# Three float16 casts at three places of ScalarE's queue, and one VectorE subtraction behind the factors of the tangent sums

## The chip, the cores and the metric

The kernel runs on one core of one Trainium2 chip. The metric is the device time of one launch in microseconds (us), of which the shorter is the better. A core has TensorE (PE in the profile, for matmuls and transposes), VectorE (DVE), ScalarE (ACT), GpSimd (POOL) and SyncE (SP, which here only issues the loads). Each takes its instructions from a queue of its own, in order[...].

## The reference, cut to what matters

Four graph layers follow each other over x (4096 nodes by 64 features) and a dense 0/1 adjacency of 4096 by 4096. Each ends in `x = layernorm(x + layer(x, adj))`. Layer 0 is a mean over neighbours with a linear map. Layer 2 is a sum over neighbours with weights that halve with each further neighbour. Layers 1 and 3 are the same hyperbolic attention:

```python
adj_att = sigmoid(left[:, None] + right[None, :] + b) * adj   # left, right: x_tan @ w
x_local = _logmap(x[:, None, :], x[None, :, :])               # 4096 x 4096 x 64
support = einsum('ij,ijd->id', adj_att, x_local)
return _proj(_expmap(x, support))
```

`_logmap` of a pair depends on x_i, x_j and their dot product. The kernel gets that dot product, together with terms of the two norms, from TensorE: a vector y (x times a factor of its norm) is split into a float16 upper half and a float16 lower half (y minus the upper half), and the products of the halves are summed in PSUM. `left` and `right` need a logarithm per node, and the sums over neighbours run over x times factors of its norm, which the kernel holds in `xe`.

## The kernel before, in words

**Tiling.** The 4096 nodes lie in 32 blocks of 128 (P). Destination columns come in four groups of 1024, walked from 3 down to 0 (`GROUPS`); source blocks come two at a time, also downwards. For each group and pair of blocks, SyncE loads 1 MB of the adjacency (L698) into one of six `edges` buffers, so that the adjacency is read once for each layer, 256 loads in all.

**Four stages.** In layer 0, TensorE sums neighbours (L1414). In layers 1 and 3 (`attend`, L1025) each pair of a block and a group has six matmuls into a PSUM tile z (L1059, L1062, L1065), a sigmoid and a square on ScalarE (L1074, L1077), two or three passes on VectorE (L1080, L1082) and, for a pair of blocks, eight matmuls into acc (L1037). Layer 2 is one wide pass over the groups 3 and 2 and then a narrow pass each for group 1 and group 0. In a narrow pass each block adds to two z tiles in place (four matmuls, L1569), ScalarE takes two exponentials of them (L1576), and four matmuls add up the result one block later (L1581). The next block's count into a z tile can't begin before the exponential has read it.

**Rows.** When a group of a layer has been summed, its 1024 rows become the next layer's x: `end_0` (L1357) or `end_2` (the function with L1494 to L1504), `norm_rows` (L862), and `prepare` (L882), the part that the change touches. `prepare` works out the norm's terms and y (L896), and leaves the rest to a generator, `second`, which is put into a queue of small steps. In its order: the three casts of y on ScalarE (L899 and L900 into two places of `ys`, L901 into `yd`); the terms of the norm in float16 (L903 to L914, on VectorE and GpSimd); the lower half of y (L915, on VectorE, which reads the result of L899); the factors and `xe` (L918 to L923); the inputs of the logarithms (L926 to L931); then four rounds that each transpose eight blocks of `ys` or `yd` into PSUM (L943) and copy them out on ScalarE (L947) as `hi_lo`, `lo_hi`, `src` and `dst`; the two logarithms (L950, L951); the product with the attention vectors (L955); and the small operations that give `left` and `right` (L965 to L977). In this text a chain is one run of `second`, named by the group of rows it works on. An attention over any destination group needs the chain of source group s only when it comes to the blocks of s.

**What sets the order.** `tick` (L614) is called between the main steps: four times for each load in layer 0, once for each block in the narrow passes. It lets the generators at the heads of two queues go on. `yield n` means: not before n ticks from now. `second` stands in the second queue, and a generator runs to its end before the next one in that queue starts:

```python
for queue in queues:
    while queue and queue[0][1] <= place[1]:
        wait = next(queue[0][0], None)
        ...
        queue[0][1] = place[1] + wait
        if wait:
            break
```

In layers 0 and 2 the main loops stand in `with tc.manual_schedule(engines=FIXED)`, where FIXED is PE and ACT: these two keep the order in which the program wrote them. VectorE and GpSimd are ordered by a list scheduler. In layers 1 and 3 it orders all engines. It also moves instructions that are written after the block of layer 2 forward into that stage: three sigmoids of layer 3's first group stand there among the exponentials of the last narrow pass. Where ScalarE goes over from exponentials to logarithms or sigmoids, or back, the built program has an ACT_TABLE_LOAD; copies, casts and squares stand among all three without one.

**PSUM.** Transposes use one `aux` tile; in layer 2 half of a third z tile serves as a second one (`take`, L667, alternates), which is given back at the end of the stage (`spare_ends`, L676).

Of the kernel before, what the change touches and what calls it, by code (L numbers as in the profile page):

```python
# [21 lines left out]
D = 64  # L22
# [36 lines left out]
def gnn_stack_kernel(  # L59
# [16 lines left out]
    V = nc.vector  # L76
# [492 lines left out]
    def stream(fits):  # L569

        with ExitStack() as st:
# [130 lines left out]
            def grp(name, bufs=None):  # L702
                kw = {"bufs": bufs} if bufs else {}
                return row.tile([P, WB, D], F32, name=name, **kw)

            def nums(name, n=WB):
                return row.tile([P, n], F32, name=name)

            def over(v):
                return v[:, :, None].to_broadcast([P, v.shape[1], D])  # L710
# [87 lines left out]
            ys = keep.tile([P, WB, 3 * D + 10], F16, name="ys")  # L798
# [83 lines left out]
            def prepare(layer, s, att, b_att, curve, least, good, small):  # L882
# [11 lines left out]
                ym, y = nums("ym"), grp("y")  # L894
# [2 lines left out]

                def second():
                    nc.scalar.copy(ys[:, :, :D], y)  # L899
                    nc.scalar.copy(ys[:, :, 2 * D : 3 * D], y)  # L900
                    nc.scalar.copy(yd[:, :, :D], y)  # L901
                    hl = row.tile([P, WB, 2], F16, name="hl")
                    V.tensor_scalar(hl[:, :, 0], rbg, UNIT, None, ALU.mult)  # L903
# [7 lines left out]
                    for k, of in ((7, 0), (8, 0), (9, 1)):  # L911
                        nc.gpsimd.tensor_scalar(
                            ed[:, :, k], hl[:, :, of], -2.0 / UNIT, None, ALU.mult
                        )  # L914
                    V.tensor_sub(ys[:, :, D : 2 * D], y, ys[:, :, :D])  # L915

                    m, g, w = nums("m"), nums("g"), grp("xw")
                    V.tensor_scalar(g, cx2[:, at], 1.0, 1.0 / D, ALU.add, ALU.mult)  # L918
# [2 lines left out]
                    V.tensor_add(w, xg, over(g))  # L921
                    yield 1
                    V.tensor_mul(xe[:, at, :], w, over(m))  # L923

                    q, q1, t = nums("q"), nums("q1"), nums("tt")
                    V.tensor_scalar(q, x2[:, at], least, c, ALU.max, ALU.mult)  # L926
# [63 lines left out]
                    yield 1  # L990

                later(second(), True, after(small))
                yield 1

# [714 lines left out]
```

## Time and profile before

| What | us |
|---|---|
| median of three runs (1107.23 to 1113.71) | 1108.87 |
| the profiled execution: its own time | 1108.28 |
| its span, first to last instruction | 1106.6 |
| busy PE, DVE, ACT, POOL | 1001.9, 915.5, 803.1, 273.1 |
| layer 0 (to about 190.6) | 190.6 |
| layer 1 (to about 517) | 326.4 |
| layer 2: wide pass, narrow pass of group 1, narrow pass of group 0 (ends at 759.28) | 110.2, 61.2, 70.9 |
| layer 3 | 347.7 |
| one cast (L899, L900, L901), eight of each | 0.62 |
| one ACT_TABLE_LOAD, 19 ahead of L950, L1074 and L1576 | 1.28 |
| lower half of y (L915), eight | 0.69 |

The time of one launch is the span plus 1.7 us around it. Times "at 737" are us from the span's start. A row of the timeline has the start, the busy time, the engine, the line, the operation with its output and input, how many instructions are merged, and in brackets the idle time of the engine ahead of it with what ended it. Rows of one engine can overlap by about 0.1 us[...].

### The profile page before, as it was taken

To read this page: it belongs to the slowest core of one execution; us is meant where nothing else is said; L and a number is where in the kernel's file an instruction comes from. 1 tells how busy PE (TensorE), PEld (TensorE's weight loads), DVE (VectorE), ACT (ScalarE), POOL (GpSimd) and SP (SyncE) were. 2 spreads that over 40 slices of the span, in tenths; PEclk is the share of its full clock that TensorE was granted. 3 is DMA by queue.
4 is the path that set the end of the run, shared out by engine and by line. 5 is a ranking of instruction groups with operands and counts; after the bars stand their busy time and mean duration, and the time that the engine had idled before them with its cause. 6 is when DMAs were issued, how large, how long until landed. Compare 5 with 4: busy or idle time off the path is not lost.

```text
span 1106.6 us, 13832 instructions
## 1 busy us (share of the span) xinstructions
PE 1001.9 (91%) x4949; PEld 392.4 (35%) x4949; DVE 915.5 (83%) x1452; ACT 803.1 (73%) x892; POOL 273.1 (25%) x649
## 2 busy tenths in 40 slices
PE   4998998889999999998998998789899999999980
PEld 2454554333333333332333332223333333333320
DVE  5777977989999999999456484545999999999996
ACT  0003123879999999897676788889899998998960
POOL 0011212010144443525500010000001444346173
PEclk8999999889999999999998999799999999999995
DMA  9999999536565565654877987477545656666400
GB/s 341 378 419 380 370 423 396 190 131 244 191 240 219 188 238 219 228 194 148 333 304 275 362 289 261 155 270 285 203 169 211 251 214 229 228 227 227 164 1 23
DMA packets 38581, 271.63 MB, mean 245 GB/s; under 512 B 4710, under 2 KB 4710, under 8 KB 5734
## 3 DMA queue, kind: packets, MB, share of 16 engines
q1 hardware_dynamic: 37728, 270.03, 64.8%
q8 instruction: 41, 0.67, 0.2%
q10 hardware_dynamic: 774, 0.63, 0.2%
q14 instruction: 38, 0.31, 0.1%
HBM read 269.58 MB, written 1.05 MB: 245 GB/s over the span
## 4 chain that ended last, share of the span: by engine, by line
PE 55%; DVE 24%; ACT 9%; DMA 5%; POOL 3%; issue 2%; ACTq 0%; SPq 0%; POOLq 0%; DVEq 0%
PE acc L1037 15%; PE z L1569 9%; DVE t L1082 7%; PE z L1059 7%; PE z L1065 6%; PE z L1062 6%; DVE t L1080 6%; DMA edges<-in_adj_dram 4%; PE acc L1581 3%; PE acc L1414 3%; ACT sq L1077 3%; ACT sq L1576 2%; DVE junk L838 2%; ACT sig L1074 1%; PE z L1581 1%
## 5 line engine op out<-in xcount | busy, mean ns | idle before, releaser
L1080 DVE SCALAR_TENSOR_TENSOR t<-z,sig 128x1024 f32<-128x1024 f32 x256 | 308.8, 1217 | 13.0 <-ACT sq L1077 6.8
L1077 ACT ACTIVATE sq<-z,turn 128x1024 f32<-128x1024 f32 x256 | 277.8, 1111 | 45.1 <-PE z L1065 18.4
L1082 DVE SCALAR_TENSOR_TENSOR t<-sq,t 128x2048 f32<-128x2048 f32 x128 | 297.3, 2322 | 0.5
L1074 ACT ACTIVATE sig<-left_b,right 128x1024 f32<-128x1024 f32 x256 | 285.9, 1146 | 1.9 <-DVE t L1080 1.3
L1037 PE MATMUL acc<-t,xe 128*64 128x512 f32 x1024 | 255.2, 608 | 17.2 <-DVE t L1082 16.8
L1059 PE MATMUL z<-edges,two_i 128*128 128x512 bf16 x512 | 201.2, 393 | 7.4 <-DVE t L1080 7.4
L1065 PE MATMUL z<-dst,src 74*128 74x512 f16 x512 | 195.5, 382 | 0.0
L1062 PE MATMUL z<-lo_hi,hi_lo 128*128 128x512 f16 x512 | 194.4, 380 | 0.0
L1576 ACT ACTIVATE sq<-z,at_edge 128x512 bf16<-128x512 f32 (+1 forms) x192 | 149.3, 828 | 46.0 <-PE z L1569 43.5
L838 DVE SCALAR_TENSOR_TENSOR t<-edges 128x2048 bf16<-128x2048 f32 x32 | 73.0, 2287 | 54.2 <-DMA edges<-in_adj_dram 54.2
L1037 PEld LDWEIGHTS acc<-t,xe 128*64 128x64 f32 x1024 | 63.8, 136 | 145.6 <-issue 83.8
L1569 PE MATMUL z<-edges,pass_by 128*128 128x512 bf16 x248 | 89.5, 401 | 17.9 <-ACT sq L1576 17.8
L1414 PE MATMUL acc<-edges,first 128*128 128x512 bf16 x256 | 80.1, 394 | 17.6 <-DMA edges<-in_adj_dram 17.3
L1059 PEld LDWEIGHTS <-two_i 128*128 128x128 bf16 x512 | 50.3, 98 | 128.9 <-issue 82.3
L1569 PE MATMUL z<-edges,enter 128*128 128x512 bf16 x256 | 91.0, 398 | 0.0
L1414 PE MATMUL acc<-edges,third 128*65 128x512 bf16 x256 | 80.0, 394 | 0.0
L838 DVE SCALAR_TENSOR_TENSOR junk<-edges 128x2048 bf16<-128x2048 f32 x32 | 73.1, 2286 | 4.7 <-DMA edges<-in_adj_dram 4.4
L1065 PEld LDWEIGHTS <-src 74*128 74x128 f16 x512 | 49.2, 96 | 70.5 <-issue 8.0
L1062 PEld LDWEIGHTS <-hi_lo 128*128 128x128 f16 x512 | 50.4, 98 | 57.1 <-issue 11.7
L1581 PE MATMUL acc<-sq,halves 128*64 128x512 bf16 x384 | 62.5, 403 | 1.0 <-ACT sums L1088 0.8
L869 POOL TENSOR_TENSOR sq<-z 128x512 f32<-128x512 f32 x8 | 14.2, 1776 | 164.3 <-DVE z L868 132.2
L1133 POOL TENSOR_TENSOR w_att<-x,u 128x512 f32<-128x512 f32 x6 | 15.6, 2595 | 141.2 <-ACT u L1128 141.2
(375 smaller groups left out, 940.9 us busy)
## 6 DMA issues: line engine op xcount, KB each, us to landing
edges<-in_adj_dram SPq DMA_DIRECT2D x256, 1024.0 KB, 4.7
x<-in_x_dram SPq DMA_DIRECT2D x4, 256.0 KB
out_dram<-x ACTq DMA_DIRECT2D x2, 256.0 KB
out_dram<-x SPq DMA_DIRECT2D x2, 256.0 KB
w_sb<-in_L_gnn_W_dram ACTq DMA_DIRECT2D x1, 32.0 KB, 4.8
w_twice<-in_L_gnn_weight_dram ACTq DMA_DIRECT2D x2, 16.0 KB, 8.6
given<-in_L_gnn_b_dram ACTq DMA_DIRECT2D x1, 0.2 KB
given<-in_L_gnn_bias_dram ACTq DMA_DIRECT2D x1, 0.2 KB
```

The source lines that it names most:

```text
L838: V.scalar_tensor_tensor(junk, a, 0.0, a, ALU.not_equal, ALU.not_equal, accum_out=odd[:, n : n + 1])
L1037: it = nc.tensor.matmul(acc[h * D : (h + 1) * D, :], xe[:, j, :], t[:, k, h * W : (h + 1) * W], start=j == BLOCKS[0], stop=j == BLOCKS[-1],)
L1059: nc.tensor.matmul(half, two_i, edge[:, at : at + W], start=True, stop=False)
L1062: nc.tensor.matmul(half, hi_lo[:, of], lo_hi[:, to], start=False, stop=False)
L1065: last = nc.tensor.matmul(half, src[:, of], dst[:, to], start=False, stop=True)
L1074: nc.scalar.activation(sig, left_b, AF.Sigmoid, bias=right[:, j : j + 1])
L1077: nc.scalar.activation(sq[:, k], zp, AF.Square, bias=turn, scale=-1.0 / UNIT)
L1080: V.scalar_tensor_tensor(t[:, k], zp, 0.0, sig, ALU.max, ALU.mult)
L1082: V.scalar_tensor_tensor(t, sq, HIGH**2, t, ALU.add, ALU.mult)
L1414: nc.tensor.matmul(accs[h][:m], lhs[:, j, :], edge[:, at : at + W], start=j == BLOCKS[0], stop=j == BLOCKS[-1],)
L1569: nc.tensor.matmul(z[:, h : h + W], lhs, rhs[:, h : h + W], start=j == BLOCKS[0], stop=True, skip_group_check=True,)
L1576: nc.scalar.activation(w, z[:, :n], AF.Exp, bias=at_edge, scale=-LN2)
```

## The change

`second` gives up its turn after each of the first two casts, so that the three casts come at three ticks rather than at one, and everything behind them comes two ticks later. The subtraction for the lower half of y is written behind the product that gives `xe`.

```diff
                 def second():
                     nc.scalar.copy(ys[:, :, :D], y)
+                    yield 1
                     nc.scalar.copy(ys[:, :, 2 * D : 3 * D], y)
+                    yield 1
                     nc.scalar.copy(yd[:, :, :D], y)
                     hl = row.tile([P, WB, 2], F16, name="hl")
                     V.tensor_scalar(hl[:, :, 0], rbg, UNIT, None, ALU.mult)
...
-                    V.tensor_sub(ys[:, :, D : 2 * D], y, ys[:, :, :D])

                     m, g, w = nums("m"), nums("g"), grp("xw")
...
                     V.tensor_add(w, xg, over(g))
                     yield 1
                     V.tensor_mul(xe[:, at, :], w, over(m))
+                    V.tensor_sub(ys[:, :, D : 2 * D], y, ys[:, :, :D])
```

No instruction is added to or taken from the source; the lines below L899 move down by one or two in the changed file. Lines in the text are those of the kernel before.

## The prediction

> **What bounds the kernel now.** The page's busy shares (PE 91%, DVE 83%, ACT 73%) are averages over stages with different limits, so I first asked for the windows of the passes of layer 2, where `prepare` runs beside exponentials, and of the first stretch of layer 3. The columns are the window, its length, and busy time with instruction counts.
>
> ```profile
> core 0: us, PE busy (x) PEld busy (x) DVE busy (x) ACT busy (x) POOL busy (x), PEclk, DMA share, GB/s
> 640.89:688.40 47.51, 42.47 (x240) 14.20 (x239) 32.41 (x113) 39.12 (x62) 5.55 (x15) 0.96 0.76 276
> 688.40:759.28 70.88, 59.07 (x334) 19.86 (x334) 28.83 (x87) 63.28 (x91) 2.39 (x8) 0.90 0.63 227
> 759.28:797.48 38.20, 34.59 (x151) 12.09 (x150) 36.66 (x66) 33.05 (x34) 1.55 (x2) 1.00 0.62 228
> ```
>
> In the pass of group 0 (second row) ScalarE is busy for 63.3 of 70.9 us and VectorE for 28.8: ScalarE and TensorE share the limit and VectorE has room. In the stretch behind it VectorE is busy for 36.7 of 38.2 us and sets the pace.
>
> Second, ScalarE's timeline at the chain of group 1:
>
> ```profile
> 735.71 1.26 ACT L1576 ACTIVATE sq<-z,at_edge 128x512 bf16<-128x512 f32 x2 [0.30 <-PE z L1569]
> 736.86 0.62 ACT L899 CAST ys<-y 128x512 f16<-128x512 f32 x1
> 737.37 0.63 ACT L900 CAST ys<-y 128x512 f16<-128x512 f32 x1
> 737.89 0.62 ACT L901 CAST yd<-y 128x512 f16<-128x512 f32 x1
> 738.41 1.27 ACT L1576 ACTIVATE sq<-z,at_edge 128x512 bf16<-128x512 f32 x2
> 739.87 1.27 ACT L1576 ACTIVATE sq<-z,at_edge 128x512 bf16<-128x512 f32 x2 [0.19 <-PE z L1569]
> ```
>
> An undisturbed block takes 1.57 us (exponentials at 734.15 and 735.71), in which ScalarE works for 1.27 and waits 0.30 for z. The three casts put 1.55 us between two blocks. On TensorE's timeline:
>
> ```profile
> 739.16 0.39 PE L1569 MATMUL z<-edges,pass_by 128*128 128x512 bf16 x1 [0.97 <-ACT sq L1576]
> ```
>
> Third, the chain of group 2's logarithms, and the end of the pass, where group 1's stand:
>
> ```profile
> 723.68 1.27 ACT L1576 ACTIVATE sq<-z,at_edge 128x512 bf16<-128x512 f32 x2
> 724.97 1.28 ACT L950 ACT_TABLE_LOAD   x1
> 726.26 0.21 ACT L950 ACTIVATE tt<-tt 128x8 f32<-128x8 f32 x1
> 726.38 0.19 ACT L951 ACTIVATE q<-q 128x8 f32<-128x8 f32 x1
> 726.59 1.28 ACT L1576 ACT_TABLE_LOAD   x1
> ```
> ```profile
> 759.29 1.28 ACT L950 ACT_TABLE_LOAD   x1
> 760.59 0.21 ACT L950 ACTIVATE tt<-tt 128x8 f32<-128x8 f32 x1
> 760.70 0.19 ACT L951 ACTIVATE q<-q 128x8 f32<-128x8 f32 x1
> 760.80 0.56 ACT L1610 COPY sums<-acc 128x512 f32<-128x512 f32 x1
> ```
>
> Inside the pass two logarithms cost two table loads, and the next exponential starts at 727.88, 4.20 us after the last instead of 1.57: 2.63 lost. At the end they come behind the last exponential, and their second load is the sigmoids', needed anyway.
>
> **What the Trainium skill says.** "ScalarE: Activation LUTs", section "What ACT_TABLE_LOAD costs", gives about 1283 ns for the load and 1380 for a drain, 2.66 us for a switch. The trace agrees on the load (1283 ns) and not on the drain: the load starts 0.02 us after the exponential, the logarithm 1.29 later, so I price a switch at 1.29. The section "Table sets: the hidden batching unit" says to batch functions by set. "Perfetto Trace Analysis", section "Optimizing Scalar/DVE Operations", says that where ScalarE causes bubbles on other engines, breaking work up may free them sooner; the 0.97 us above is such a bubble. "TensorE: Matmul & The Clock Gate", section "What's actually happening", has a gate pass only part of the clock by how busy TensorE has been. The granted clock was 0.75 in 700 to 720, behind the three hoisted sigmoids.
>
> **The change part by part.** I read the order of the built programs, engine by engine.
>
> *VectorE's subtraction: 0.* It costs 0.69 us wherever it stands. The list scheduler already put it behind `xe` in layer 0 (L923 at 84.95, L915 at 85.64). Its one stall, 3.69 us on L899 at 737.5, fell where VectorE had work for 28.8 of 70.9 us. Its cover gone, it would cost up to 0.69 per chain, bounds 0 and +0.7 (only the last chain, in layer 3, lies where VectorE is full).
>
> *Layer 0: 0, bounds -2 and +2.* DMA is 0.96 busy up to 190.6. Group 3's `lo_hi` copy (1.01) moves behind the four copies of sums, and group 2's rows no longer wait 1.62 us for the logarithm at 105.7. SyncE's loads do wait for L838 on VectorE, so the cover isn't perfect. Layer 1's order and the last three groups of layer 3 are unchanged, and so are the orders on POOL and SP: no DMA is moved past anything.
>
> *Casts, three chains in layer 2: -1.4.* One block apart, each of three blocks takes 1.27 + 0.52 = 1.79, 0.22 over 1.57: 0.66 for three. Group 1 lost 1.02 before (2.70 and 1.46 for two blocks, less 2 x 1.57): gain 0.36. Group 2's casts lie among table loads, where ScalarE never waits: 1.27 + 1.55 + 2 x 1.57 = 5.96 becomes 3 x 1.79: gain 0.6. Group 3 lost 1.8, of it 0.66 waiting for y, which stays, then 0.22 twice: gain 0.5. Bounds: -3.5 (all of it hidden) and 0. In layer 3 the scheduler keeps the casts together: 0.
>
> *The queue: six blocks.* Chains follow each other in one queue, so the two ticks add up: group 3's ends two blocks later, group 2's four, group 1's begins four and ends six later. Before, group 1's chain left the pass with its last block. Now it begins eight blocks ahead of the end, and two of its copies, its logarithms and L955 are written behind the manual block. The scheduler moves the two logarithms forward, singly: load, L950, load, one block, load, L951, load, with the last three blocks still to come behind. Each is 1.28 + 0.2 + 1.28, say 2.85 with the start-up, less 0.30 of idle time: 2.5. Two: +5.0. Bounds: +4.2 (one more idle gap hidden each) and +5.3 (2.63 each).
>
> *TensorE's clock behind them: +1.2.* After the logarithms at 669 the next blocks took 1.85 and 2.49, 1.2 over, with matmuls at 0.63 instead of 0.39; after those at 726 nothing. Two interruptions one block apart resemble the sigmoids at 689 to 705, which were followed by a dip. Bounds 0 and +2.4; I take one dip.
>
> *Transposes that leave the pass: -1.4.* A block with transposes took 2.05 us (exponentials at 748.71 and 750.76): 0.48 over. Three of group 1's four rounds now fall at or behind the last block. Bounds -1.4 and 0, since they go into layer 3.
>
> *The end of the pass: 0.* From the last exponential's end (759.28) to the first L1080 (762.82) it was 3.54. Now the sums' copy can start when acc is done (+0.95, so +1.5), but the `lo_hi` copy (0.9) must free the one `aux` tile before the transposes of the sums (0.6) and L1494 (0.34): about 3.5 again. Bounds -1 and +1.5.
>
> *VectorE in layer 3: +0.9.* L965, L968, L975 to L977, L983, L988 and L989 of group 1 stood at 758.9 to 762.2, beside the wait; now they stand between L1080s: eight times about 0.11. Bounds 0.6 and 1.2, unless L965 has to wait (rival B).
>
> *Group 0's chain in layer 3: +0.5.* Casts and copies come two squares earlier, and the table load for its logarithms catches VectorE with one sigmoid in hand rather than two. Bounds -1 and +2.
>
> Sum: -1.4 + 5.0 + 1.2 - 1.4 + 0.9 + 0.5 = +4.8. On the profiled execution, 1108.28 (span 1106.6 and 1.7 around it), that is 1113.1; on the median, 0.6 higher, 1113.7, which I give.
>
> **Rivals.**
>
> B, the other side of the line, slower at 1118: L965 waits on VectorE for L955, which waits for the `dst` copy to free `aux`, behind two squares, a table load, a sigmoid, the `src` copy and a square on ScalarE. I place that at 10.7 us behind the last exponential, and VectorE gets there at 11.4. Past 0.7 us of delay each us is paid in full, since all L1080s queue behind L965; a trip of transpose and copy more (0.6 + 0.9), twice, gives 3, with a second dip 4.2: 1113.7 + 4.2. For it: one tile where there were two. Against: ScalarE had 5 us of idle time up to 797.
>
> C, a gain: the moved work is hidden, the casts free their whole 3.5 and layer 0 gains 2, while the loads cost 4.2: 1107. For it: L838 holds loads. Against: the 2.63 at 726, measured in this very place.
>
> D, the change doesn't do what it says: spreading frees nothing and the logarithms' loads are absorbed by the six blocks' freedom: 1109. Against: ScalarE's built order has three more table loads in a pass where it is 89% busy.
>
> **How the numbers follow.** Chances: my forecast A 0.50, B 0.20, C 0.15, D 0.15. Anything within 0.5% (5.5 us) can't be told from no change by a measurement of this kernel. A spreads over 1110 to 1117 and lies beyond 1114.4 with 0.18 of its 0.50. Slower: 0.18 + 0.20 = 0.38. Faster: 0.04 of C and 0.01 of D, 0.05. Within: 0.57. The range from 1107.5 to 1119 leaves out most of C's gains and B's tail.
>
> **What would show it.** Right: ten table loads in the last narrow pass become thirteen; two gaps of about 2.3 us on L1569; no gap of 0.97 at the casts; the pass of group 0 longer by 3 to 5 us, layers 0 and 1 unchanged. Wrong: the loads cost under 1 us each on TensorE, VectorE idles at L965, or layer 0 ends at another time by over 2 us.

## The result, and the profile after

The changed kernel takes 1123.26 us, the median of six runs (1116.48 to 1125.64), beside 1108.22 for the kernel before. The ratio of the two sets of runs is 1.0111, 95% interval 1.0084 to 1.0138, or some 12 us; the quotient of the two medians alone would be 1.0136. I had forecast 1113.7 and a range up to 1119. The profiled execution, one of the quicker of the six, has 1118.83, 10.55 more than the 1108.28 of before, and its span is 1117.1: the stretches below account for these 10.5 us, not for the whole distance of the medians. A later comparison of the same kernel gave 1.0109 (1.0070 to 1.0148).

To say where the time went I cut both spans at three events that every trace has: the copy of the wide pass's sums in layer 2, the end of the last exponential, and the copy of layer 3's first sums.

| Stretch, us | before | after | difference | my forecast |
|---|---|---|---|---|
| start to the wide pass's sums | 625.51 | 623.09 | -2.4 | 0 |
| the two narrow passes, to the last exponential | 133.77 | 137.84 | +4.1 | +3.4 |
| from there to layer 3's first sums | 92.18 | 98.13 | +5.9 | +1.4 |
| the rest of layer 3 | 255.14 | 258.04 | +2.9 | 0 |
| span | 1106.6 | 1117.1 | +10.5 | +4.8 |

The narrow passes went as I had worked out, and the stretch behind them did not. First, ScalarE's timeline at the logarithms of group 1, which answers to the third block of the prediction (start, busy time, operation, idle time before it). Rows carry the line numbers of the file that ran: in the changed kernel L952, L953, L967, L1496 and L1578 are L950, L951, L965, L1494 and L1576 of the kernel before.

```profile
744.43 1.30 ACT L1578 ACTIVATE sq<-z,at_edge 128x512 bf16<-128x512 f32 x2
745.76 1.28 ACT L952 ACT_TABLE_LOAD   x1
747.05 0.21 ACT L952 ACTIVATE tt<-tt 128x8 f32<-128x8 f32 x1
747.28 1.28 ACT L1578 ACT_TABLE_LOAD   x1
748.57 1.27 ACT L1578 ACTIVATE sq<-z,at_edge 128x512 bf16<-128x512 f32 x2
749.86 1.28 ACT L953 ACT_TABLE_LOAD   x1
751.15 0.21 ACT L953 ACTIVATE q<-q 128x8 f32<-128x8 f32 x1
751.38 1.28 ACT L1578 ACT_TABLE_LOAD   x1
752.67 1.27 ACT L1578 ACTIVATE sq<-z,at_edge 128x512 bf16<-128x512 f32 x2
754.12 1.27 ACT L1578 ACTIVATE sq<-z,at_edge 128x512 bf16<-128x512 f32 x2 [0.18 <-PE z L1571]
757.38 1.48 ACT L1578 ACTIVATE sq<-z,at_edge 128x512 bf16<-128x512 f32 x2 [1.99 <-PE z L1571]
...
759.65 1.28 ACT L1578 ACTIVATE sq<-z,at_edge 128x512 bf16<-128x512 f32 x2
```
```profile
749.31 0.39 PE L1571 MATMUL z<-edges,pass_by 128*128 128x512 bf16 x1 [2.36 <-ACT sq L1578]
753.41 0.39 PE L1571 MATMUL z<-edges,pass_by 128*128 128x512 bf16 x1 [2.36 <-ACT sq L1578]
```

Each of the two interruptions holds TensorE for 2.36 us, and two blocks behind the second ScalarE waits 1.99 us for z. The windows of the last narrow pass, of the stretch up to group 0's y, and of the pass's last 8.9 us show the granted clock (the number before the DMA share): it has fallen to 0.81 at the end of the pass, and the matmuls of the z that ScalarE waits for take 0.63 us instead of 0.39.

```profile
core 0: us, PE busy (x) PEld busy (x) DVE busy (x) ACT busy (x) POOL busy (x), PEclk, DMA share, GB/s
684.27:760.93 76.66, 59.89 (x304) 19.39 (x308) 29.89 (x100) 67.07 (x95) 3.14 (x8) 0.89 0.62 210
760.93:800.27 39.34, 36.63 (x165) 13.37 (x167) 34.64 (x62) 33.02 (x33) 1.51 (x2) 0.96 0.63 224
752.00:760.93 8.93, 7.52 (x41) 2.85 (x40) 0.16 (x1) 6.63 (x10) 0.00 (x0) 0.81 0.49 175
```

The second row answers to the third of the prediction's first block: the stretch has grown from 38.2 to 39.3 us, and VectorE works in it for 34.6 us where it worked for 36.7 (one pass of L1082, 2.2 us, now comes behind y). VectorE's timeline at the end of the pass, first before:

```profile
761.82 0.16 DVE L976 TENSOR_TENSOR right<-lr,f 128x8 f32<-128x8 f32 x1
...
762.15 0.42 DVE L1494 SCALAR_TENSOR_TENSOR z<-aux,given_b 128x256 f32<-128x256 f32 x1
762.49 0.41 DVE L1498 SCALAR_TENSOR_TENSOR z<-aux,given_b 128x256 f32<-128x256 f32 x1
762.82 1.21 DVE L1080 SCALAR_TENSOR_TENSOR t<-z,sig 128x1024 f32<-128x1024 f32 x1
...
810.14 0.21 DVE L965 TENSOR_REDUCE lr<-aux 128x16 f32<-128x48 f32 x1
```

and then after, with one row of GpSimd:

```profile
764.59 0.42 DVE L1496 SCALAR_TENSOR_TENSOR z<-aux,given_b 128x256 f32<-128x256 f32 x1 [12.43 <-PE aux L1097]
764.93 1.22 DVE L1082 SCALAR_TENSOR_TENSOR t<-z,sig 128x1024 f32<-128x1024 f32 x1
766.07 0.41 DVE L1500 SCALAR_TENSOR_TENSOR z<-aux,given_b 128x256 f32<-128x256 f32 x1
...
773.09 1.08 POOL L869 TENSOR_TENSOR sq<-z 128x512 f32<-128x512 f32 x1 [48.58 <-DVE lr L967]
773.18 1.01 DVE L978 TENSOR_TENSOR right<-lr,f 128x8 f32<-128x8 f32 x1
...
813.44 0.21 DVE L967 TENSOR_REDUCE lr<-aux 128x16 f32<-128x48 f32 x1 [2.64 <-PE aux L957]
```

Of the 12.43 us, 3.66 lie behind the last exponential (760.93). In the kernel before, nine small operations of group 1 (L970 to L977, L988, L989), L1494 and L1498 filled 2.0 of the 3.54 us up to the first product. In the changed kernel four of the nine are done inside the pass, and the other five stand between the products, as does L1500 (L1498 before). One of the five, L978, takes 1.01 us where it took 0.16 (L976 before); it ends with the GpSimd row beside it. The second hole, 2.64 us, is in group 0's chain, and the kernel before has none there (its L965 at 810.14 follows without a gap). TensorE's timeline behind y, first before, then after:

```profile
800.44 0.61 PE L943 MATMUL aux<-ident,ys 128*128 128x128 f16 x8
800.89 0.39 PE L1059 MATMUL z<-edges,two_i 128*128 128x512 bf16 x1
...
802.15 0.61 PE L943 MATMUL aux<-ident,ys 128*128 128x128 f16 x8 [0.44 <-ACT hi_lo L947]
802.74 1.93 PE L1037 MATMUL acc<-t,xe 128*64 128x512 f32 x6
...
805.17 1.07 PE L1037 MATMUL acc<-t,xe 128*64 128x512 f32 x2
```
```profile
801.78 0.62 PE L945 MATMUL aux<-ident,ys 128*128 128x128 f16 x8 [1.70 <-DVE ys L925]
803.50 1.01 PE L945 MATMUL aux<-ident,ys 128*128 128x128 f16 x8 [1.10 <-ACT hi_lo L949]
804.45 1.97 PE L1039 MATMUL acc<-t,xe 128*64 128x512 f32 x2
806.35 1.07 PE L945 MATMUL aux<-ident,ys 128*74 128x128 f16 x8
807.35 2.89 PE L1039 MATMUL acc<-t,xe 128*64 128x512 f32 x6
```

The first rounds of transposes now stand with no z matmuls between them, TensorE waits, and what follows is slower: eight transposes take 1.01 to 1.07 us instead of 0.61, and the eight matmuls of acc, in two pieces, 1.97 and 2.89 us instead of 1.07 and 1.93.

### The profile page after: what moved, and what is told of

Same layout as the page of the kernel before. It is cut to its first block, busy times and chain, and to the rows that moved or that the text cites. A ratio compares the mean times of both kernels' runs of the same rounds, so it can differ in the third digit from the quotient of the medians.

```text
span 1117.1 us, 13749 instructions
## 1 busy us (share of the span) xinstructions
PE 1006.0 (90%) x4863; PEld 396.0 (35%) x4949; DVE 916.9 (82%) x1452; ACT 808.1 (72%) x895; POOL 273.2 (24%) x649
## 4 chain that ended last, share of the span: by engine, by line
PE 57%; DVE 24%; ACT 9%; issue 3%; DMA 3%; POOL 3%; ACTq 0%; SPq 0%; POOLq 0%; DVEq 0%
PE acc L1039 16%; PE z L1571 9%; DVE t L1084 7%; PE z L1064 7%; PE z L1061 6%; PE z L1067 6%; DVE t L1082 6%; PE acc L1583 4%; PE acc L1416 3%; ACT sq L1578 3%; DVE junk L838 3%; ACT sq L1079 2%; DMA edges<-in_adj_dram 2%; PE z L1583 1%; ACT sig L1076 1%
## 5 line engine op out<-in xcount | busy, mean ns | idle before, releaser
L1082 DVE SCALAR_TENSOR_TENSOR t<-z,sig 128x1024 f32<-128x1024 f32 x256 | 308.7, 1217 | 13.3 <-ACT sq L1079 7.4
L1039 PE MATMUL acc<-t,xe 128*64 128x512 f32 x1024 | 261.1, 615 | 17.3 <-DVE t L1084 16.8
L1061 PE MATMUL z<-edges,two_i 128*128 128x512 bf16 x463 | 181.4, 392 | 4.4 <-DVE t L1082 4.4
L1578 ACT ACTIVATE sq<-z,at_edge 128x512 bf16<-128x512 f32 (+1 forms) x192 | 150.1, 830 | 46.6 <-PE z L1571 43.3
L1416 PE MATMUL acc<-edges,first 128*128 128x512 bf16 x241 | 77.2, 396 | 18.3 <-DMA edges<-in_adj_dram 17.9
L1571 PE MATMUL z<-edges,enter 128*128 128x512 bf16 x241 | 86.5, 402 | 0.5
L1583 PE MATMUL acc<-sq,halves 128*64 128x512 bf16 x384 | 62.7, 404 | 2.8 <-issue 1.8
L869 POOL TENSOR_TENSOR sq<-z 128x512 f32<-128x512 f32 x8 | 15.1, 1883 | 161.3 <-DVE z L868 92.9
```

The lines of the kernel that those rows point to most:

```text
L1039: it = nc.tensor.matmul(acc[h * D : (h + 1) * D, :], xe[:, j, :], t[:, k, h * W : (h + 1) * W], start=j == BLOCKS[0], stop=j == BLOCKS[-1],)
L1061: nc.tensor.matmul(half, two_i, edge[:, at : at + W], start=True, stop=False)
L1082: V.scalar_tensor_tensor(t[:, k], zp, 0.0, sig, ALU.max, ALU.mult)
L1416: nc.tensor.matmul(accs[h][:m], lhs[:, j, :], edge[:, at : at + W], start=j == BLOCKS[0], stop=j == BLOCKS[-1],)
L1571: nc.tensor.matmul(z[:, h : h + W], lhs, rhs[:, h : h + W], start=j == BLOCKS[0], stop=True, skip_group_check=True,)
L1578: nc.scalar.activation(w, z[:, :n], AF.Exp, bias=at_edge, scale=-LN2)
```

## The experiments

The theory with which I went on, Q: the spreading is harmless, and the two ticks that each chain is late cost the time, through group 1's logarithms in the pass (first term) and through VectorE's and group 0's order in layer 3 (second term). The rivals: S, the casts between the exponentials break TensorE's run; K, only the clock of the runs differs. Each kernel below was timed beside the kernel before. The table has the ratio with its interval, and from one profiled execution of each the stretches of the table above: N (narrow passes), L (to layer 3's first sums), R (the rest).

| Kernel | ratio (95%) | N | L | R | span |
|---|---|---|---|---|---|
| before | 1 | 133.77 | 92.18 | 255.14 | 1106.6 |
| changed | 1.0111 (1.0084, 1.0138) | 137.84 | 98.13 | 258.04 | 1117.1 |
| spread_only | 0.9994 (0.9977, 1.0011) | 131.91 | 93.18 | 255.13 | 1109.2 |
| delay_only | 1.0054 (1.0037, 1.0071) | 134.56 | 97.98 | 257.38 | 1111.8 |
| layer0_only | 0.9992 (0.9972, 1.0011) | 133.79 | 92.18 | 255.08 | 1106.3 |
| layer2_only | 1.0101 (1.0070, 1.0133) | 135.26 | 96.70 | 256.98 | 1111.6 |
| yields_only | 1.0078 (1.0053, 1.0103) | 135.27 | 96.70 | 257.00 | 1115.1 |
| group1_late | 1.0051 (1.0032, 1.0070) | 135.30 | 95.73 | 255.95 | 1113.1 |
| one_log | 1.0034 (1.0018, 1.0051) | 134.18 | 95.95 | 257.32 | 1115.4 |
| late_read | 1.0088 (1.0057, 1.0118) | 137.79 | 98.50 | 256.97 | 1118.6 |
| spaced | 1.0112 (1.0087, 1.0137) | 136.24 | 96.22 | 257.08 | 1113.8 |
| logs_end | 1.0028 (1.0010, 1.0047) | 131.97 | 95.70 | 256.10 | 1106.4 |
| one_inside | 1.0059 (1.0031, 1.0087) | 134.56 | 96.04 | 257.22 | 1110.7 |
| logs_apart | 1.0079 (1.0050, 1.0108) | 134.77 | 96.88 | 258.11 | 1112.5 |
| changed_beside | 1.0109 (1.0070, 1.0148) | 138.43 | 98.00 | 257.96 | 1117.5 |
| sigmoids_end | 0.9930 (0.9903, 0.9957) | 122.03 | 95.64 | 256.36 | 1097.7 |
| spread_sigmoids_end | 0.9892 (0.9867, 0.9917) | 120.72 | 94.69 | 255.08 | 1096.1 |

The time up to the wide pass's sums, left out here, lies between 621.9 and 629.0 us and follows no edit: 625.25 with the yields in layer 0 alone, 622.66 with layer 0 as before.

### Spreading, delay and place taken apart

**spread_only**

```diff
                     yield 1        # between the casts, as in the change
...
-                    yield 1
                     V.tensor_add(w, xg, over(g))
-                    yield 1
                     V.tensor_mul(xe[:, at, :], w, over(m))
```

> Casts at three ticks as in the change, but the two later yields of the same generator (ahead of the sum and of the product that give xe) are taken out, so that everything behind the casts keeps its place in the queue. TensorE's order is that of the kernel before, and ScalarE's differs only in the casts of groups 3, 2 and 1 in layer 2. Theory Q (the two ticks by which the queue is late cost the time): 0 to 3 us less than before, ratio about 0.999. Theory S (the casts between the exponentials cost it): 6 to 10 us more than before, most of it in the narrow passes. Theory K (only a lower granted clock of the runs): within 3 us of before at the same clock.

No change that can be measured, so S falls. The passes are 1.86 us shorter, as Q says; the 1.0 us more in L has the same built order as before, and the granted clock in the 20 us behind y was 0.91 in this profile and 1.00 in that of before. The 1.86 us are not the casts' alone, though: two of the three sigmoids among the exponentials come two blocks later in this built order. Over the last 26 exponentials of the pass, which hold group 1's casts and no sigmoid, the gain is 0.82 us (22.75 instead of 23.57).

**delay_only**

```diff
+                    yield 1
+                    yield 1
                     nc.scalar.copy(ys[:, :, :D], y)
-                    yield 1
                     nc.scalar.copy(ys[:, :, 2 * D : 3 * D], y)
-                    yield 1
                     nc.scalar.copy(yd[:, :, :D], y)
```

> The two yields stand ahead of the three casts, which stay together: the same delay of two ticks a chain, no spreading. TensorE's order is that of the changed kernel; in the last narrow pass ScalarE's two logarithms of group 1 stand together (one interruption, not two). Theory Q: 7 to 10 us more than before: the changed kernel's loss, less 2.6 for the one interruption, plus 1.4 for the casts; VectorE again waits 2 to 3 us for group 0's product with the attention vectors in layer 3. Theory S: within 2 us of before. Theory K: within 3 us of before at the same clock.

Slower by 4.1 to 7.9 us, a little under Q's 7 to 10. The wait for group 0's product is there (2.73 us), and L is as long as in the changed kernel. N is only 0.8 over before: one interruption instead of two, and a clock of 0.99 in the pass's last 10 us.

**layer0_only** and **layer2_only**: the two `yield 1` stand under `if layer == 1:` or under `if layer == 3:` (the layer whose rows the chain prepares).

> The change with the yields taken only in layer 0's chains (those of layer 1's rows); layer 2 as before. Theory Q, as the profile has it: layer 0 ends about 2.2 us earlier and nothing else changes, 2 us less than before. If the earlier end of layer 0 was chance (my prediction's 0): the same as before, with layer 1's first sums at 289 us. Theory S: in layer 0 ScalarE is idle most of the time, so 0.

> The change with the yields taken only in layer 2's chains (those of layer 3's rows); layer 0 as before. Theory Q: 12 to 13 us more than before in the profiled execution (the 10.5 measured plus the 2.2 that layer 0 no longer gains), with the 2.6 us wait of VectorE for group 0's product in layer 3 there again. Theory K: as the changed kernel, within 1 us.

Layer 0's part is nothing, and the 2.4 us in the first row of my table were chance: layer 1's first sums came at 288.69 us. The loss is all in layer 2's chains. The profiled execution of layer2_only was by far the quickest of its six (1113.3, the others from 1118.2 to 1122.8), so that its span, 5.0 us over before where I expected 12 to 13, says little; the ratio does. It shows one thing: with the same order its N is 2.6 us shorter than the changed kernel's, and the clock in the last 10 us of its pass was 1.00.

**yields_only**: the kernel before with the two yields; the subtraction stays where it was.

> The change without its second part: the casts at three ticks, the subtraction written where it was before. TensorE's and ScalarE's orders are those of the changed kernel; VectorE's differs only in a few rows of layer 0. Theory Q: as the changed kernel within 1 us, 12 to 15 us more than before. Rival V (the subtraction behind xe holds back group 0's transposes in layer 3, which wait 1.7 us for it): 1.7 us less than the changed kernel or more.

It is 5.9 to 11.4 us over before, less than Q's 12 to 15; its interval overlaps that of the changed kernel. Its N and L are those of layer2_only, in which the subtraction stands behind xe, to 0.01 us: the subtraction's place is no part of them. V falls: TensorE waits for `ys` in this place too, 1.96 us.

**group1_late**: two ticks for one chain.

```diff
+                    if (layer, s) == (3, 1):
+                        yield 2
                     nc.scalar.copy(ys[:, :, :D], y)
```

> The kernel before, with one wait of two ticks ahead of group 1's three casts in layer 2 and nothing else (the subtraction is written behind xe, which leaves VectorE's order as it was): two ticks of delay rather than six, no spreading. In the built order group 1's logarithms then interrupt the pass once, one copy of group 1 instead of two falls behind the pass's end, and group 0's transposes in layer 3 stand close together as in the changed kernel. Theory Q: +2.6 for the interruption, and +3 to +5 in layer 3 if group 0's order costs it: 5 to 8 us more than before. Rival T (the cost grows with the ticks): two of six ticks, 3 to 4 us more, and no wait of VectorE for group 0's product in layer 3.

Two ticks cost as much as delay_only's six: 3.5 to 7.8 us, with the one interruption (N +1.5) and a wait of 2.2 us for group 0's product (L +3.6). T falls: it is not the number of ticks but which side of the pass's end group 1's last steps are on.

### The interruptions of the pass

**one_log**: the logarithm of 1 - q1 is taken as that of 1 + (-q1), beside that of 1 + t.

```diff
-                    q, q1, t = nums("q"), nums("q1"), nums("tt")
+                    q = nums("q")
+                    lg = row.tile([P, 2, WB], F32, name="lg")
+                    t, q1 = lg[:, 0, :], lg[:, 1, :]
...
-                    V.tensor_scalar(q1, q1, QTOP, None, ALU.min)
+                    V.tensor_scalar(q1, q1, QTOP, -1.0, ALU.min, ALU.mult)
...
-                    nc.scalar.activation(t, t, AF.Ln, bias=1.0)
-                    nc.scalar.activation(q1, q1, AF.Ln, bias=1.0, scale=-1.0)
+                    nc.scalar.activation(lg, lg, AF.Ln, bias=1.0)
```

> The changed kernel with the inputs of the two logarithms side by side in one tile (the second one negated on VectorE), so that one ACTIVATE takes both. TensorE's order is that of the changed kernel but for one pair of instructions in layer 3; ScalarE's differs in that group 1's logarithms interrupt the last narrow pass once instead of twice. Theory Q: one interruption is worth 2.5 us and up to 1.2 of clock behind it: 2.5 to 4 us less than the changed kernel, 8 to 10 us more than before. Rival A (the second interruption is hidden in ScalarE's idle time, and the loss is all in layer 3): as the changed kernel within 1 us.

2.0 to 5.7 us over before, where Q had 8 to 10: more than half of the loss is gone with one of two interruptions, at least twice what I had put on it. That raised the question of what the second costs, and the next ones answer it with ScalarE's logarithms moved and nothing else: the built orders of TensorE and VectorE are those of the changed kernel.

`exps` is a list of the exponentials' instructions. The diff is that of **one_inside**. **logs_end** has the same for the first logarithm too, **logs_apart** has `exps[-5]` in the place of `exps[-1]`, and **changed_beside** is the changed kernel once more.

```diff
-                    nc.scalar.activation(q1, q1, AF.Ln, bias=1.0, scale=-1.0)
+                    log = nc.scalar.activation(q1, q1, AF.Ln, bias=1.0, scale=-1.0)
+                    if (layer, s) == (3, 1):
+                        in_order(log.ins, exps[-1].ins)
```

> The changed kernel with group 1's two logarithms ordered behind the last exponential of the pass, where the kernel before had them. TensorE's order is the changed kernel's, ScalarE's differs in these two and their table loads alone. Theory Q (two terms: the interruptions in the pass, and group 0's chain with VectorE's idle time in layer 3): from the wide pass's sums to the last exponential 131 to 133 us (137.8 and 135.3 in the changed kernel's profiles), layer 3 as in the changed kernel with its wait of 2.4 to 2.7 us, together 3 to 6 us less than the changed kernel and 5 to 9 more than before. Rival L (the loss is all in layer 3): as the changed kernel within 1.5 us.

> The changed kernel with the second of group 1's logarithms ordered behind the last exponential: one interruption in the pass, one at its end in the place of a load that is needed anyway. Theory N: 2.5 us less than the changed kernel. Theory D: 4 to 7 us less than the changed kernel, near the 4 us over before of the kernel with one logarithm.

> The changed kernel with the second of group 1's logarithms two blocks later, so that the two interruptions of the last narrow pass stand three blocks apart rather than one; the order of everything else is the changed kernel's. Theory N (each interruption costs what it takes, wherever it stands): as the changed kernel within 1.5 us. Theory D (two of them one block apart make TensorE's clock fall, and blocks between them prevent it): 2 to 4 us less than the changed kernel.

> The changed kernel itself on the same chip as the other two: 9 to 13 us more than before.

A ladder of ratios: no interruption 1.0028, one 1.0059, two three blocks apart 1.0079, two one block apart 1.0109 and 1.0111. Neighbours overlap in their intervals; the two ends do not, so rival L falls. The steps between are not measured singly: one_log, with one interruption as well, has 1.0034. And logs_end is only 1.1 to 5.2 us over before, where Q had 5 to 9, with a wait of 1.5 us for group 0's product. What an interruption costs is read in its place, from the start of the twelfth-last exponential to the end of the last one; both logarithms of the changed kernel fall into these six blocks.

| Interruptions in them | kernel | us | clock |
|---|---|---|---|
| none | logs_end | 10.09 | 1.00 |
| one | one_inside, one_log | 12.62, 12.63 | 1.00 |
| two, three blocks apart | logs_apart | 14.70 | 1.00 |
| two, one block apart | yields_only, layer2_only | 15.15, 15.16 | 1.00 |
| two, one block apart | changed, changed_beside, late_read | 16.50, 16.55, 16.44 | 0.90 |
| two, one block apart | spaced | 16.29 | 0.79 |

So one interruption costs 2.5 us and two cost 4.6 to 5.1, as N says. The fall of the clock that D speaks of comes on top, with 1.1 to 1.4 us, in four of six profiles of one and the same order, and in none of the others: D's place for it is right, but it is one of two outcomes. ScalarE's timeline of logs_end at the end of the pass (its L1583 is L1576 of the kernel before):

```profile
749.24 1.26 ACT L1583 ACTIVATE sq<-z,at_edge 128x512 bf16<-128x512 f32 x2 [0.30 <-PE z L1575]
751.26 1.26 ACT L1583 ACTIVATE sq<-z,at_edge 128x512 bf16<-128x512 f32 x2 [0.76 <-PE z L1575]
...
753.31 1.29 ACT L1583 ACTIVATE sq<-z,at_edge 128x512 bf16<-128x512 f32 x2
754.61 1.28 ACT L952 ACT_TABLE_LOAD   x1
```

Blocks follow each other at 1.57 to 2.05 us to the end, with no wait of 2 us for z, and the load stands behind the last exponential, as before the change. The window of the pass's last 9 us in the same kernel, with the clock third from the right:

```profile
745.60:754.60 9.00, 9.00 (x58) 3.09 (x57) 0.00 (x0) 7.34 (x12) 0.00 (x0) 1.00 0.87 310
```

**sigmoids_end** applies the price to the kernel before, which already had three sigmoids of layer 3 among the exponentials. `before` is the base here, and **spread_sigmoids_end** has spread_only as its base.

```diff
-                        nc.scalar.activation(
+                        one = nc.scalar.activation(
                             sig, left_b, AF.Sigmoid, bias=right[:, j : j + 1]
                         )
+                        if layer == 3 and s == GROUPS[0]:
+                            in_order(one.ins, exps[-1].ins)
```

> The kernel before with the sigmoids of layer 3's first group ordered behind the last exponential: the three that stood among the exponentials, with two table loads each, go there, and six table loads less one are gone. A test of the price of an interruption on the kernel before. Theory P (2.5 us each, and the clock behind them): the last narrow pass 7 to 9 us shorter, VectorE's first product of layer 3 some 2 to 3 us later behind the last exponential, together 4 to 7 us less than before. Rival H (ScalarE's work only moves: the three sigmoids are missing when layer 3 begins, and VectorE, which sets the pace there, pays in full): within 2 us of before.

> The kernel that spreads the casts without delay, with the sigmoids behind the last exponential as well: the candidate for the best of both. Theory P and the 1.9 us that spreading alone took from the passes: 5 to 9 us less than before. Rival H: within 2 us of before.

Both are faster than both kernels: 5 to 11 us under before for the first, where P had 4 to 7, and 9 to 15 us (1.1%) for the second, where P had 5 to 9. H falls. The windows of the last narrow pass, from the copy of its predecessor's sums to the last exponential, first of before and then of sigmoids_end (clock third from the right):

```profile
687.35:759.28 71.93, 59.59 (x336) 19.97 (x336) 28.83 (x87) 64.33 (x92) 2.39 (x8) 0.91 0.64 230
```
```profile
684.33:745.70 61.37, 56.17 (x330) 19.19 (x336) 28.98 (x87) 53.24 (x83) 4.74 (x8) 0.97 0.75 270
```

The pass is 10.6 us shorter, where P had 7 to 9. ScalarE lost nine instructions and 11.1 us of work. TensorE, with all 336 weight loads still there, is busy for 3.4 us less at a clock of 0.97 rather than 0.91; six of its matmuls have no record in this trace, so that part of the 3.4 may be theirs. Layer 3 begins 3.5 us slower (L), which is what H had seen.

### Group 0's chain in layer 3

**late_read**: VectorE's first read of the product, `read`, is ordered behind the twelfth following product of sigmoid and z (`in_order(read.ins, one.ins)`).

> The changed kernel with VectorE's first read of group 0's product with the attention vectors in layer 3 put behind a later product of sigmoid and z (the twelfth after the place where it is written), so that VectorE has some 3.5 us of other work where it waits 2.6 us in the changed kernel. Theory B (this wait is paid in full): 2 to 2.6 us less than the changed kernel. Theory G (the wait is only where a stretch of TensorE at half clock shows; VectorE, let go earlier, then waits for TensorE's z instead): 0 to 1 us less.

L is 98.50 us, no shorter than 98.13. VectorE no longer waits at the product but for the squares:

```profile
815.17 0.16 DVE L722 SCALAR_TENSOR_TENSOR rt<-rs_t,rt 128x8 f32<-128x8 f32 x1
816.62 1.22 DVE L1084 SCALAR_TENSOR_TENSOR t<-z,sig 128x1024 f32<-128x1024 f32 x1 [1.28 <-ACT sq L1081]
```

In all it waits 4.9 us for squares up to layer 3's first sums, where the changed kernel waits 2.1. B, as an isolated wait that is paid in full, falls in this profile; G's "only where it shows" holds. The ratio alone couldn't say so: 1.0088 is 2.5 us below the 1.0111 of the changed kernel, which is B's figure, but the intervals overlap over most of their length.

**spaced**: the first transpose for `lo_hi` of group 0 is ordered behind the z matmul of the thirteenth following block.

> The changed kernel with group 0's transposes for lo_hi in layer 3 ordered behind the z matmuls of a later block, so that TensorE has z matmuls between two rounds of transposes, as in the kernel before, where the changed kernel has none and runs at half clock. Theory G (TensorE, idle between the rounds of transposes, runs at half clock, and VectorE's 2.6 us are its shadow): no half clock in the 10 us behind y, from y to layer 3's first sums 55 to 57 us where the changed kernel has 58.7, 2 to 3 us less than the changed kernel. Rival O (the few microseconds are VectorE's idle time at the end of the pass, whatever the order of the chain): from y to the sums 58 to 59 again.

G's forecast failed: VectorE doesn't wait at the product, and yet the clock in the first 10 us behind y is 0.69 and 0.63, and from y to the sums it is 58.2 us. That is O's figure, but not O's reason: of the 4.0 us that L has over before, VectorE's idle time up to y makes 2.0, and the rest comes behind y. The run is no clean test of what z matmuls between the rounds would do, as TensorE waits twice for nearly 2 us before the first of them comes:

```profile
800.02 0.70 PE L945 MATMUL aux<-ident,ys 128*128 128x128 f16 x8 [1.96 <-DVE ys L925]
802.69 3.68 PE L1041 MATMUL acc<-t,xe 128*64 128x512 f32 x8 [1.97 <-DVE t L1089]
```

Setting one pair of instructions right doesn't bring back the old order's time.

## Why the prediction was wrong

*What was right.* Layers 0 and 1 at 0 (layer0_only), and the subtraction at 0 (yields_only). The three further loads, singly, each holding TensorE for 2.36 us. The interruptions at +5.0: the last six blocks take 5.06 us more in yields_only than in logs_end, both at a clock of 1.00 (four blocks followed the second logarithm, not the three that I had counted). The clock dip at +1.2: 1.1 to 1.4 where it came; that it came in this profile was one of two outcomes, since two of six profiles of this order have none. The end of the pass at 0 with bounds -1 to +1.5: from the last exponential to the first product it is 4.00 us instead of 3.54.

*What was right in direction.* The casts at -1.4: group 1's gained 0.82 us (spread_only), where I had 0.36; my working for group 3 gives 0.7 and not the 0.5 that I entered. The transposes that leave the pass, at -1.4: the last 20 exponentials take 17.77 us in spread_only, with all four rounds among them, and 16.63 in logs_end, with the first two and the three casts, both at a clock of 1.00. Over both passes the two kernels are level at 131.9 us, because the clock in the last pass up to its twelfth-last exponential was 0.89 in the first and 0.86 in the second. Such differences of the clock may also hide the casts' gain between delay_only (together) and one_inside (apart), which both take 134.56 us.

*The step that failed* is the stretch behind the pass, and in it above all "group 0's chain in layer 3", at +0.5 with bounds -1 and +2. With "VectorE in layer 3" at +0.9 I had +1.4 for the stretch; it measured +5.9 in the profile of the changed kernel, and 3.5 to 6.3 in all kernels in which group 1's chain is late. VectorE's books show where. They run from the last exponential over the same 35 products (L1080) and 17 passes over a pair of blocks (L1082) in each kernel (these end 2.0 to 2.1 us behind the start of the sums' copy); each instruction counts until the next one of the engine begins.

| VectorE, us | before | changed | yields_only |
|---|---|---|---|
| up to the first product | 3.54 | 4.00 | 3.82 |
| the products and the passes over pairs | 77.8 | 77.8 | 77.8 |
| small operations among them | 10.8 | 12.9 | 12.8 |
| idle behind the first product | 2.0 | 5.5 | 4.4 |

- The small operations: group 1's eight cost 1.5 us in their new place, not 0.9, because L978 takes 1.01 us beside GpSimd's square. In group1_late it takes 0.16, and the eight cost 0.6. L1500, which now stands behind the first product, adds 0.3. So the way of pricing (what they take where they go) was right, and two entries were missing.
- The idle time: +3.5 us, where I had +0.5 for group 0's chain and nothing for a lower clock behind the pass. In the changed kernel 1.0 of it lies ahead of y, with a clock of 0.96 (0.0 in yields_only, at 1.00). From y to the sums it is 1.92 us before and 4.51 after. That is rival B's wait (2.64 us at L967), but at group 0's chain, where I hadn't looked, not at group 1's, where I had placed it. I had read that the built order of group 0's chain changes and priced the table load in it alone. late_read and spaced show that it is no single wait: it moves to other instructions, with TensorE at 0.6 to 0.7 of its clock.

How far the new order causes this and how far the clock does stays open. From y to the sums, VectorE's idle time goes with the clock in the 20 us behind y. In the old order it is 1.9 us at 1.00 (before, layer0_only, spread_sigmoids_end) and 2.8 at 0.91 (spread_only, sigmoids_end). With a late chain it is 3.2 to 3.7 at 0.91 (logs_end, group1_late, one_inside, one_log) and 3.8 to 4.7 at 0.83 (the others); no late chain has 1.00. With one profile of each it is not shown whether the order lowers the clock.

*A term that I had mis-sized* as a whole: the interruptions over the entire run. logs_end against the changed kernel is 1.0028 against 1.0111, about 9 us, of which the passes hold about 6. The rest lies in L (95.70 against 98.13) and R (256.10 against 258.04), where the built orders of TensorE and VectorE are the same. In the profile of changed I can name the windows in which the clock is lower (0.96 up to y, 0.83 in the 20 us behind it, against 1.00 and 0.91 in logs_end; 0.88 in the last 10 us of layer 3's fourth and last group, against 1.00), but not why an interruption some 10 to 330 us earlier should do that. The last of these dips, 1.3 us of R, comes without the interruptions too: sigmoids_end, with neither them nor a late chain, has 0.83 there. The rest stays open. So does the share of a late chain in R: 0.85 us are lost in layer 3's second group in every kernel with a changed order of group 0's chain, and not in spread_only.

*The range* ended at 1119 because I let B cost at most 4.2 us on top of my forecast and took its place to be one wait. The profiled execution, 1118.83, lies just inside it, and the median of the six, 1123.26, does not; no profile shows what the four slower ones spent more.

## What to carry to other kernels

A delay of a few steps in a side queue is not priced by its length: two ticks on one chain cost as much as six, because what counts is whether the chain's last steps still end beside the wait that hid them. Price work that leaves a wait at what it takes in its new place, beside what runs there, and then ask which waits the new order opens behind it: here they were the larger part. And where an engine changes function tables inside a tight loop, put the odd functions together behind the loop: "Table sets: the hidden batching unit" in the Trainium skill's page "ScalarE: Activation LUTs" says to batch functions by table set, and here the three sigmoids that stood among exponentials in both kernels were worth 0.7% when they were held back to the pass's end.

## What the runs showed of the hardware

- An interruption of ScalarE by one function of another table set, with its two table loads, held TensorE for 2.36 us and cost 2.5 us of the pass; two of them cost 4.6 us three blocks apart and 5.1 us one block apart. One block apart, the clock over the last six blocks was 1.00 in two profiles (yields_only, layer2_only) and 0.79 to 0.90 in four (changed, changed_beside, late_read, spaced), for 1.1 to 1.4 us more; ScalarE's longest wait for z there was 0.86 us in the two and 1.39 to 2.11 us in the four.
- That fits the page "TensorE: Matmul & The Clock Gate", section "What's actually happening", in that the gate follows how busy TensorE has been. The order of the instructions alone doesn't tell when it will: with the same built order from the pass's end to layer 3's first sums, the clock in the 20 us behind group 0's y was 1.00 in before and 0.91 in spread_only.
- An operation of VectorE on 128x8 elements took 1.01 us beside GpSimd's product of 128x512 (L978 beside L869, in the changed kernel) and 0.16 us without it.
- The time of a run goes with its mean clock: the changed kernel's six went from 1116.48 us at 0.962 to 1125.64 at 0.953, and their mean clock was 0.957 where the kernel before had 0.966 over 49 runs. So a single profile can be 4.4 us off the median of its own kernel, and 6.7 us in layer2_only.
